# Attention units with key blocks turned by VectorE and DMA: another sharing-out of copies, exponentials and scores

## The chip, the cores and the metric

The kernel runs on one core of a Trainium2 chip. The core has a matrix engine (TensorE, "PE" in the profile, with "PEld" for its weight loads), VectorE ("DVE"), ScalarE ("ACT"), GpSimd ("POOL") and SyncE ("SP"), which here issues every DMA. Each engine works through its own instructions in program order; semaphores tie them together. TensorE writes to PSUM, eight banks of 512 float32 columns on 128 partitions; VectorE and ScalarE read it back.

The metric is the device time of one execution in microseconds (us). Before the change the median of three runs is 2802.39 us (2792.26 to 2804.34).

## What is computed

An encoder layer over a context of 77 tokens, then a decoder layer over x, which has 2 batches of 2048 tokens with 512 channels. The change concerns the decoder's causal self-attention with 16 heads of 32 channels:

```python
yn = _ln(y, dec_n1_s, dec_n1_b)
y = y + _mha(yn, yn, dec_sa_in_w, dec_sa_in_b, dec_sa_out_w, dec_sa_out_b, sb)
...
scores = jnp.einsum('bhqd,bhkd->bhqk', q, k) / jnp.sqrt(jnp.asarray(hd, xq.dtype))
scores = scores + bias[None]
attn = jax.nn.softmax(scores, axis=-1)
out = jnp.einsum('bhqk,bhkd->bhqd', attn, v)
```

`sb` is a relative-position bias plus a causal mask; keys after the query have no weight. Everything is float32.

## The kernel before

The self-attention is cut into 128 **units** (b, m, g, t): batch b (2), token block m of 512 (4), head group g of four heads (4), query tile t of 128 (4), in this order. A unit has n = 4m + t + 1 key blocks of 128. These are grouped into *pieces* of at most four blocks (`pieces`, L315). For each piece the following happens:

- **Scores** (`scores`, L391). Four matmuls, one per head, into four PSUM banks (L409). VectorE evicts each into the large buffer `pp` and takes a running maximum (L422; L429 for the two blocks near the diagonal, with the bias). After a unit's last piece one reduction (L439) gives the negative maxima `nm`, and four exponentials, one per head over the unit's whole width, are put on a list, `late_exps`. They are issued later by `exps(k)` (L364) on ScalarE (L444, in place, with a sum).
- **Turning** (`turn`, L450). The probabilities have queries on the partitions; for the product with the values the keys must be there. TensorE transposes each key block's four heads into one bank (L466), and VectorE (L474) or ScalarE (L476) copies the bank into one of the `pts` tiles.
- **Values** (`values`, L483). One matmul per key block and head (L503) adds up the unit's output in one bank, which is then copied (ScalarE, L517) or added (VectorE, L519) to `oT`.

Units for which `moved(n)` (L332) holds turn their first piece (the *far* one, four key blocks) in another way. These are all units of m = 3 and of block (1, 2), but for the last two of all. `move_out` (L378) transposes squares of 32 x 32 within `pp` on VectorE, with two instructions (L383) that cover the four heads, and writes the result to DRAM with two DMAs (L384, tensor `turn`). `move_in` (L386) reads it back with four DMAs (L389) into `landing`, the upper half of `pts_all`, in an order that completes the transposition. `move(n)` calls `move_out` and gives the space free for later scores. TensorE does not transpose these four blocks.

The order of work is written out by hand in the loop at the end of `tile_encoder_decoder`. It goes through the units and, within a unit, through its *visits* (`visits_of`, L336): one or two pieces of a unit that isn't moved; one piece of a moved one, with the far blocks' values in the last visit. So a moved unit of m = 3 has three visits and one of (1, 2) has two. In a visit the loop turns the piece, runs at the unit's end the next `slot` (projections, norms and output products of neighbouring blocks, weight loads, GpSimd work), moves the next unit's far piece out (`early`), issues exponentials, scores up to two pieces of units n + 1 and n + 2, and then the values; the landing DMAs come last. `stream` lists the pieces still to be scored, in order; `may_score` tells whether the next one's space in `pp` is free. Units of even and odd number use opposite ends of `pp`, so unit n + 2 writes where unit n was.

PSUM banks are handed out in a ring (`bank`, eight banks); `values` takes the oldest one for its sums and puts it back at the end. So a matmul may have to wait for the eviction of whatever used the bank eight calls earlier.

Which engine copies a turned bank is decided by `half` (L470 to L472): in a moved unit of m = 3 the fourth copy of a piece (o == 3) goes to VectorE; in one of (1, 2) the second half of each piece; all others to ScalarE. The exponentials of the next unit are issued for m = 3 as two in the first visit, two in the second and none in the third; for (1, 2) all four in the first visit.

After the attention, `ff_slot` and `cross` run the cross-attention and the feed-forward layers, whose matmuls (L1686, L1715 and others) fill the rest of the time.

Of the kernel before, what the change touches and what calls it, by code (L numbers as in the profile page):

```python
# [22 lines left out]
HC = P // HD  # L23
MB = 512
NMB = T // MB
# [29 lines left out]
def tile_encoder_decoder(ctx: ExitStack, tc: tile.TileContext, ins, out):  # L55
# [103 lines left out]
    with (  # L159
# [169 lines left out]
        units = [(b, m, g, t) for b in range(B) for m in range(NMB) for g in range(NC) for t in range(TB)]  # L329
        stream = [(n, k0, kn) for n, u in enumerate(units) for k0, kn in pieces(u[1] * TB + u[3])]  # L330

        def moved(n):  # L332

            return (units[n][1] == NMB - 1 or units[n][:2] == (1, 2)) and n < len(units) - 2

        def visits_of(n):  # L336

# [26 lines left out]
        def exps(k):  # L364

            for _ in range(min(k, len(late_exps))):
                late_exps.pop(0)[1]()
# [82 lines left out]
        def turn(pieces):  # L450

            first = units[pieces[0][0]][1] == 0
            loads = []
            for n, k0, kn in pieces:
                ks = range(k0, k0 + kn)
                if first:
                    heads = [(n, k, r) for r in range(HC) for k in ks]
                    loads += [heads[o : o + TB] for o in range(0, len(heads), TB)]
                else:
                    loads += [[(n, k, r) for r in range(HC)] for k in ks]  # L460
            for o, load in enumerate(loads):
                pt = bank()
                pts = in_turn("pts4", pts_all[:, :HC]) if moved(pieces[0][0]) else in_turn("pts", pts_all)
                pts = pts.rearrange("p (x q) -> p x q", q=P)
                for x, (n, k, r) in enumerate(load):
                    nc.tensor.transpose(pt[:, ts(x, P)], state[n]["p"][r][:, k], ident)  # L466
                    got[n, k, r] = pts[:, x, :]
                w = len(load) * P
                free = pieces[0][0] == len(units) - 2 and (pieces[0][1] or o >= 4)
                half = o >= (len(loads) + 1) // 2  # L470
                if moved(pieces[0][0]) and units[pieces[0][0]][1] == NMB - 1:
                    half = o == 3  # L472
                if free or (o % 2 if first else o in (4, 6) if len(loads) == 8 else half):
                    nc.vector.tensor_copy(pts[:, : len(load), :], pt[:, :w])  # L474
                else:
                    nc.scalar.copy(pts[:, : len(load), :], pt[:, :w])  # L476
                if not first and o == (7 if len(loads) == 8 else min(3, len(loads) - 1)):
                    exps(1)
            exps(HC if first else 0 if units[pieces[0][0]][1] == NMB - 1 else 1)

        sums_held = {}

        def values(n, turned, far, opens, ends):  # L483
            b, m, g, t = units[n]
            for k0, kn in far:
                parts = landing.rearrange("p a (r k x) -> p r k a x", r=HC, x=RB)
                for k in range(kn):
                    for r in range(HC):
                        got[n, k0 + k, r] = parts[:, r, k]
            ks = [k for k0, kn in turned + far for k in range(k0, k0 + kn)]  # L490
            whole = m == 0
            key = (b, m, g) if whole else n
            begun = key in sums_held
# [1436 lines left out]
        def score_next():  # L1930
            score_at()
            at[0] += 1
# [29 lines left out]
        for n, visit, turned, far in ((n, k, *w) for n in range(end) for k, w in enumerate(visits_of(n))):  # L1962
            pair = [(n, *p) for p in turned]
            while scored_to[n] != size[n]:
                score_next()
            while any(u == n for u, _ in late_exps):
                exps(1)
            ends = visit == len(visits_of(n)) - 1
            if moved(n) and n not in gone:
                move(n)  # L1970
                move_in(n)
            turn(pair)
            if n == end - 2:
                for _, k0, _ in pair:
                    feed(k0 + 4)
            leave(n, turned)
            turned_to[n] += sum(kn for _, kn in turned)
            third = units[n][1] == 2
            if third and ends:
                exps(2)  # L1980
            if ends and n + 1 < end:
                slot(n + 1)
            early = ends and n + 1 < end and moved(n + 1)
            early = early and scored_to[n + 1] == size[n + 1] and not any(u == n + 1 for u, _ in late_exps)
            if early:
                move(n + 1)
            if not third:
                exps((0, 2, 1, 1)[units[n][1]])
            if moved(n):
                for _ in range(2):  # L1990
                    if may_score() and stream[at[0]][0] <= n + 2:
                        score_next()
            elif may_score():
                if units[n][1] and (len(pair) > 1 or third):
                    score_two()
                else:
                    score_next()
            if third and not ends:
                exps(1)
            values(n, turned, far, visit == 0, ends)  # L2000
            if early:
                move_in(n + 1)
            while not moved(n) and may_score() and (len(pair) > 1 or units[n][1] == 0):
                score_next()
            if third and not ends:
                exps(1)
# [68 lines left out]
```

## Time and profile before

| | |
|---|---|
| median of three runs | 2802.39 us |
| the profiled execution: its time / its span | 2802.98 us / 2801.1 us |
| TensorE busy | 2725.2 us (97%) |
| VectorE busy | 1893.3 us (68%) |
| ScalarE busy | 1483.3 us (53%) |
| copies of turned banks on ScalarE (L476) / on VectorE (L474) | 614 / 290 |
| moving out: VectorE transposes (L383) / DMAs out / DMAs in | 92 / 92 / 184 |
| granted TensorE clock, mean | 0.989 |

A row of a group reads: line, engine, operation, output <- input, shape, count | busy us, mean ns of one | idle us of that engine just before these instructions, and what ended most of it. "DVE pp L422" as a releaser means VectorE's instruction of line 422 that writes `pp`. A matmul's busy time includes its place in the pipeline; a full PE row is therefore not yet a TensorE at its peak. In the view of stretches each row gives a window in us from the span's start, its length, then busy us (and instructions) of PE, PEld, DVE, ACT and POOL, the granted TensorE clock, the DMA engines' share and GB/s. In a timeline a row gives start us, length us, engine, line, operation and count, and in brackets the idle time before it with its releaser. In the view of waits it is who <- for whom: us in total, times, longest.

### The profile page before, as it was taken

How to read it: one execution, taken by the hardware profiler on the slowest of the kernel's cores; microseconds unless marked ns; L12 is line 12 of the kernel's file. 1: busy time of each engine (PE TensorE's matmuls, PEld its weight loads, DVE VectorE, ACT ScalarE, POOL GpSimd, SP SyncE). 2: the span in 40 equal slices, each digit the busy share in tenths (PEclk: the TensorE clock that was granted, in tenths of full speed). 3: DMA queues.
4: the chain of work that ended last, by engine and by line, in shares of the span. 5: the costliest groups of instructions: out<-in, count | busy, mean ns of one | idle time of the engine just before them, and what ended most of it. 6: DMA issues, size and time to landing. Idle time of an engine off the chain costs nothing. (4 is left out here: it accounts for less than half of the span.)

```text
span 2801.1 us, 67173 instructions
## 1 busy us (share of the span) xinstructions
PE 2725.2 (97%) x25870; PEld 2172.0 (78%) x25870; DVE 1893.3 (68%) x5481; ACT 1483.3 (53%) x2878; POOL 1000.8 (36%) x844
## 2 busy tenths in 40 slices
PE   9999999999999999988989999999999999999998
PEld 5678777766666677766666767898989898989898
DVE  4776688878885677778888785464655655564645
ACT  3545567756676556745556676435343444444431
POOL 3512145400301513313300011374647474747455
PEclk9999999999999999999999999999999999999999
DMA  8735355435555522368874565574758575757575
GB/s 236 209 90 148 110 176 162 134 105 161 173 163 157 146 70 75 109 197 243 248 192 143 149 192 181 167 245 142 241 145 243 165 235 159 225 161 222 147 226 184
DMA packets 347792, 481.50 MB, mean 172 GB/s; under 512 B 45600, under 2 KB 170064, under 8 KB 347346
## 3 DMA queue, kind: packets, MB, share of 16 engines
q1 hardware_dynamic: 347474, 477.22, 57.8%
q8 instruction: 205, 3.36, 0.5%
q14 instruction: 113, 0.93, 0.1%
HBM read 382.39 MB, written 94.71 MB: 170 GB/s over the span
## 5 line engine op out<-in xcount | busy, mean ns | idle before, releaser
L444 ACT ACTIVATE pp<-pp,nm 128x128 f32<-128x128 f32 (+15 forms) x512 | 611.7, 1200 | 53.6 <-DVE nm L439 50.6
L422 DVE TENSOR_SCALAR_CACHE_REDUCE pp<-psum 128x512 f32<-128x512 f32 (+3 forms) x1024 | 555.1, 590 | 58.4 <-DMA turn<-pp 30.3
L476 ACT COPY pts<-psum 128x512 f32<-128x512 f32 x614 | 328.6, 594 | 386.1 <-PE psum L466 353.7
L466 PE MATMUL psum<-ident,pp 128*128 128x128 f32 x3616 | 461.8, 280 | 8.3 <-ACT nT L310 4.0
L466 PEld LDWEIGHTS psum<-ident,pp 128*128 128x128 f32 x3616 | 398.7, 143 | 67.1 <-issue 36.0
L409 PE MATMUL psum<-kT,q 32*128 32x512 f32 (+3 forms) x2560 | 402.2, 566 | 10.2 <-DVE pp L422 3.9
L503 PEld LDWEIGHTS psum<-pts,vv 128*32 128x32 f32 x8704 | 229.1, 112 | 182.5 <-DVE pp L422 86.1
L503 PE MATMUL psum<-pts,vv 128*32 128x128 f32 x8704 | 298.6, 281 | 37.2 <-DVE pp L422 31.2
L1715 PE MATMUL psum<-pp 128*128 128x128 f32 x2560 | 304.5, 276 | 1.9 <-POOL pp L1010 1.6
L1715 PEld LDWEIGHTS psum<-pp 128*128 128x128 f32 x2560 | 296.3, 192 | 8.6 <-issue 3.0
L409 PEld LDWEIGHTS psum<-kT,q 32*128 32x128 f32 x2560 | 172.9, 184 | 148.8 <-issue 53.5
L1010 POOL TENSOR_TENSOR pp<-pp 128x512 f32<-128x512 f32 x159 | 212.6, 1353 | 112.0 <-ACT pp L862 45.5
L1686 PE MATMUL psum<-vv,pp 128*128 128x256 f32 x1024 | 236.2, 381 | 0.0
L474 DVE COPY pts<-psum 128x512 f32<-128x512 f32 x290 | 191.5, 685 | 61.1 <-PE psum L466 60.5
L1686 PEld LDWEIGHTS psum<-vv,pp 128*128 128x128 f32 x1024 | 190.3, 190 | 25.8 <-issue 0.5
L429 DVE CUSTOM_DVE_ANT_0 pp<-psum,bias 128x256 f32<-128x256 f32 (+1 forms) x512 | 195.6, 410 | 16.6 <-PE psum L409 16.6
L1699 DVE TENSOR_TENSOR kT<-kT,psum 128x512 f32<-128x512 f32 x96 | 65.8, 687 | 191.1 <-PE psum L1686 190.9
L1686 PE MATMUL psum<-nT,pp 128*128 128x256 f32 x768 | 174.1, 380 | 0.0
L1702 ACT ACTIVATE kT<-kT,vecs 128x256 f32<-128x256 f32 x192 | 87.0, 501 | 156.6 <-DVE kT L1699 155.9
L542 POOL TENSOR_TENSOR oT<-rirows,oT 128x512 f32<-128x512 f32 x30 | 38.4, 1280 | 361.1 <-DMA rirows<-rec 245.4
L1686 PEld LDWEIGHTS psum<-nT,pp 128*128 128x128 f32 x768 | 144.2, 190 | 20.3 <-issue 1.6
L1723 ACT COPY oT<-psum 128x128 f32<-128x128 f32 x56 | 15.0, 268 | 238.8 <-PE psum L1715 238.8
(273 smaller groups left out, 4229.3 us busy)
## 6 DMA issues: line engine op xcount, KB each, us to landing
pp<-w_d SPq DMA_DIRECT2D x520, 256.0 KB
turn<-pp SPq DMA_DIRECT2D x92, 512.0 KB
pts<-turn SPq DMA_DIRECT2D x184, 256.0 KB
pp<-in_dec_ff_wT_dram SPq DMA_DIRECT2D x112, 256.0 KB
bias<-tzg SPq DMA_DIRECT2D x128, 128.0 KB
pp<-wo_d SPq DMA_DIRECT2D x56, 256.0 KB
wqk<-in_dec_sa_in_wT_dram SPq DMA_DIRECT2D x52, 256.0 KB
wqk<-sa_q SPq DMA_DIRECT2D x84, 128.0 KB
```

What stands on the lines that cost most here:

```text
L409: nc.tensor.matmul(banks[r][:, : kn * P], q[rows4(r), ts(t, P)], kT[rows4(r), g, k0 * P : (k0 + kn) * P], start=True, stop=True,)
L422: nc.vector.tensor_scalar(to, got_s, 1.0, None, ALU.mult, ALU.max, accum_out=st["mx"][:, r, c : c + 1],)
L429: nc.vector.tensor_tensor_reduce(p[:, k0 + far : i + 1], s[:, far:kn], near[:, 2 - (kn - far) :], 1.0, LOWEST, ALU.add, ALU.max, accum_out ...
L444: nc.scalar.activation(p, p, AF.Exp, bias=nm, accum_out=to)
L466: nc.tensor.transpose(pt[:, ts(x, P)], state[n]["p"][r][:, k], ident)
L474: nc.vector.tensor_copy(pts[:, : len(load), :], pt[:, :w])
L476: nc.scalar.copy(pts[:, : len(load), :], pt[:, :w])
L503: nc.tensor.matmul(o if len(p.shape) == 2 else o.rearrange("p (a x) -> p a x", x=RB), vv[:, k, ts(g * HC + r, HD)], p, start=k == ks[0] an ...
L1010: engine.tensor_tensor(out, a, b, ALU.subtract)
L1686: nc.tensor.matmul(mm[:, ts(f, TOK)], a[:, c, ts(f, P)], b[:, c, :], start=fresh and f == 0 and c == 0, stop=c == 1, skip_group_check=True,)
L1702: nc.scalar.activation(dst[:, e, :], src[:, e, :], AF.Relu, bias=vec("dec_ff1_b", f + e))
L1715: nc.tensor.matmul(psum[:, bank_i, ts(col, P)], lhs[:, c, :], w[:, c, :], start=fresh and k in (0, 3) and c == 0, stop=c == 3, skip_group_ ...
```

## The change

Four units are no longer moved (`OPEN`: the first two of block (0, 3) and the first two of block (1, 2)). In moved units ScalarE copies every turned bank (`half = False`). A visit's values take the far blocks first. In a moved unit's visits the loop has a branch of its own: exponentials go one per visit from `turn`, with the rest (`exps(HC)`) at the unit's end, and in (1, 2) one more behind each visit's values; if the next piece to score is a unit's first, its second goes ahead of it where space allows; the next unit's far piece is moved out before these scores in (1, 2) and after them at m = 3. A unit that isn't moved but precedes a moved one (`then`) moves that one's far piece out just before its own values.

```diff
+        OPEN = ((0, NMB - 1, 0, 0), (1, 2, 0, 0))
+
         def moved(n):
 
-            return (units[n][1] == NMB - 1 or units[n][:2] == (1, 2)) and n < len(units) - 2
+            b, m, g, t = units[n]
+            return (m == NMB - 1 or (b, m) == (1, 2)) and n < len(units) - 2 and (b, m, g, t // 2) not in OPEN
...
-                if moved(pieces[0][0]) and units[pieces[0][0]][1] == NMB - 1:
-                    half = o == 3
+                if moved(pieces[0][0]):
+                    half = False
...
-            exps(HC if first else 0 if units[pieces[0][0]][1] == NMB - 1 else 1)
+            exps(HC if first else 0 if units[pieces[0][0]][1] == NMB - 1 or moved(pieces[0][0]) else 1)
...
-            ks = [k for k0, kn in turned + far for k in range(k0, k0 + kn)]
+            ks = [k for k0, kn in far + turned for k in range(k0, k0 + kn)]
...
+            if moved(n):
+                if ends:
+                    exps(HC)
+                    slot(n + 1)
+                early = ends and moved(n + 1)
+                if early:
+                    assert scored_to[n + 1] == size[n + 1] and not any(u == n + 1 for u, _ in late_exps)
+                if early and third:
+                    move(n + 1)
+                for _ in range(2):
+                    if at[0] == len(stream) or stream[at[0]][0] > n + 2:
+                        break
+                    if stream[at[0]][1] == 0 and may_score(1) and stream[at[0] + 1][0] == stream[at[0]][0]:
+                        stream[at[0] : at[0] + 2] = stream[at[0] + 1], stream[at[0]]
+                    if may_score():
+                        score_next()
+                if early and not third:
+                    move(n + 1)
+                values(n, turned, far, visit == 0, ends)
+                if early:
+                    move_in(n + 1)
+                if third:
+                    exps(1)
+                continue
...
-            if moved(n):
-                for _ in range(2):
-                    if may_score() and stream[at[0]][0] <= n + 2:
-                        score_next()
-            elif may_score():
+            if may_score():
...
+            then = ends and not early and n + 1 < end and moved(n + 1) and scored_to[n + 1] == size[n + 1]
+            if then and not any(u == n + 1 for u, _ in late_exps):
+                early = True
+                move(n + 1)
             values(n, turned, far, visit == 0, ends)
...
-            while not moved(n) and may_score() and (len(pair) > 1 or units[n][1] == 0):
+            while may_score() and (len(pair) > 1 or units[n][1] == 0):
                 score_next()
```

One unit of m = 3 (unit 53) as the loop writes it out before and after. T4 is the turning of key block 4, with A or D for the copying engine; E54 an exponential of unit 54; S55[4+4] the scores of unit 55's four blocks from the fourth on; V the values; OUT and IN the moving:

```
before: T4A T5A T6A T7D E54 E54 S55[0+4] S55[4+4] V | T8A T9A T10A T11D E54 E54 S55[8+4] V | T12A T13A slot OUT54 S55[12+4] V IN54
after:  T4A T5A T6A T7A E54 S55[4+4] S55[0+4] V | T8A T9A T10A T11A E54 S55[8+4] V | T12A T13A E54 E54 slot S55[12+4] OUT54 V IN54
```

And one of (1, 2) (unit 101):

```
before: T4A T5A T6D T7D E102 E102 S103[0+4] S103[4+4] E102 V E102 | T8A T9D slot OUT102 S103[8+4] V IN102
after:  T4A T5A T6A T7A E102 S103[4+4] S103[0+4] V E102 | T8A T9A E102 slot OUT102 S103[8+4] V IN102 E103
```

## The prediction

> **What bounds the kernel now.** First the page's head and its slices, to see where TensorE is not full:
>
> ```profile
> PE 2725.2 (97%) x25870; PEld 2172.0 (78%) x25870; DVE 1893.3 (68%) x5481; ACT 1483.3 (53%) x2878; POOL 1000.8 (36%) x844
> PE   9999999999999999988989999999999999999998
> DVE  4776688878885677778888785464655655564645
> ```
>
> TensorE dips below nine tenths in slices 18, 19 and 21 of 40 (1190 to 1470 us, a slice being 70 us), with VectorE at seven and eight tenths. From the 26th on (about 1750 us) it is full to the end: feed-forward matmuls, which can only start when the attention is over, so what the attention saves or loses moves the end one for one. The attention has 128 units (one L439 per unit); I cut the span at every fourth or sixteenth L439. The view of stretches gives, in order: block (0,2), whose units move nothing; the first four units of (0,3); its next eight; the first four of (1,2); its other twelve; block (1,3).
>
> ```profile
> core 0: us, PE busy (x) PEld busy (x) DVE busy (x) ACT busy (x) POOL busy (x), PEclk, DMA share, GB/s
> 362.30:578.20 215.90, 215.80 (x2600) 168.14 (x2598) 177.72 (x608) 157.21 (x274) 94.74 (x79) 1.00 0.51 149
> 578.20:658.00 79.80, 72.97 (x795) 52.44 (x794) 59.88 (x186) 47.98 (x71) 1.27 (x1) 0.96 0.42 121
> 658.00:801.20 143.20, 138.72 (x1622) 97.17 (x1621) 118.63 (x379) 101.60 (x157) 28.21 (x22) 1.00 0.60 172
> 1197.50:1262.00 64.50, 54.63 (x577) 39.61 (x577) 48.96 (x150) 33.25 (x55) 10.19 (x9) 0.92 0.65 198
> 1262.00:1445.30 183.30, 165.05 (x1786) 119.62 (x1785) 156.80 (x481) 98.88 (x168) 49.51 (x39) 0.94 0.81 235
> 1445.30:1658.90 213.60, 203.69 (x2373) 145.10 (x2372) 174.32 (x550) 140.77 (x208) 18.96 (x15) 0.98 0.58 164
> ```
>
> Blocks (0,2) and (1,2) have the same tokens, heads and keys, and (1,2) spares TensorE the turning of 4 key blocks in each unit. Yet it takes 64.5 + 183.3 = 247.8 us against 215.9. Where blocks are moved, VectorE is the fullest engine that does not pipeline: 156.80 of 183.3 (86%), 118.63 of 143.2 (83%). The groups of the same stretches (first the eight units of (0,3), then the twelve of (1,2)) say what fills it and what TensorE waits for:
>
> ```profile
> L422 DVE TENSOR_SCALAR_CACHE_REDUCE pp<-psum 128x512 f32<-128x512 f32 (+3 forms) x112 | 64.2, 628 | 5.8 <-DMA turn<-pp 4.6 <-PE psum L409 1.2
> L444 ACT ACTIVATE pp<-pp,nm 128x1664 f32<-128x1664 f32 (+3 forms) x32 | 58.9, 1849 | 3.6 <-DVE nm L439 3.6
> L476 ACT COPY pts<-psum 128x512 f32<-128x512 f32 x68 | 35.6, 597 | 33.1 <-PE psum L466 31.6 <-ACT pp L444 0.9 <-ACT oT L517 0.6
> L474 DVE COPY pts<-psum 128x512 f32<-128x512 f32 x16 | 11.0, 685 | 1.8 <-PE psum L466 1.8
> L383 DVE STREAM_TRANSPOSE pp<-pp 128x1024 f32<-128x1024 f32 x16 | 18.9, 1220 | 0.9 <-ACT pp L444 0.9
> L503 PEld LDWEIGHTS psum<-pts,vv 128*32 128x32 f32 x928 | 23.7, 109 | 19.2 <-DVE pp L422 10.2 <-issue 6.8 <-ACT pts L476 2.2
> ...
> L422 DVE TENSOR_SCALAR_CACHE_REDUCE pp<-psum 128x512 f32<-128x512 f32 (+3 forms) x124 | 68.8, 607 | 16.3 <-DMA turn<-pp 12.3 <-PE psum L409 2.4 <-PE psum L466 1.7
> L444 ACT ACTIVATE pp<-pp,nm 128x1152 f32<-128x1152 f32 (+3 forms) x48 | 67.6, 1410 | 10.0 <-DVE nm L439 8.5 <-DMA turn<-pp 1.5
> L476 ACT COPY pts<-psum 128x512 f32<-128x512 f32 x41 | 22.4, 584 | 57.8 <-PE psum L466 49.5 <-DVE pp L383 4.2 <-issue 4.0
> L474 DVE COPY pts<-psum 128x512 f32<-128x512 f32 x36 | 23.6, 684 | 2.8 <-PE psum L466 2.8
> L429 DVE CUSTOM_DVE_ANT_0 pp<-psum,bias 128x256 f32<-128x256 f32 x48 | 18.7, 417 | 0.0
> L383 DVE STREAM_TRANSPOSE pp<-pp 128x1024 f32<-128x1024 f32 x24 | 28.3, 1219 | 0.6 <-ACT pp L444 0.6
> ```
>
> The values (L503) wait for VectorE's evictions of scores (L422), and VectorE itself stands still until the DMA that carries moved blocks out has read the space it writes to (12.3 us of 183.3).
>
> **The change, part by part.** The sum is made against the profiled execution, 2802.98 us (span 2801.1; the median of three runs is 2802.39, lowest 2792.26).
>
> *(a) All copies of turned pieces to ScalarE.* Going through the loop visit by visit, L474 falls from 290 copies to 199 and L476 rises from 614 to 721; in the 42 units still moved VectorE loses 98. That is 8 per four units of blocks m = 3 (11.0 / 2 = 5.5 us of VectorE) and 12 per four of (1,2) (23.6 / 3 = 7.9 us). ScalarE gains 8 x 0.597 = 4.8 and 12 x 0.584 = 7.0 us.
> [...]
>
> *(b) Scores in another order.* When a unit's first piece is next, its second goes ahead, so the eviction into moved-out space comes one piece (four L422 of 607 ns, 2.4 us) later. The waits of the whole run, with count and longest:
>
> ```profile
> DVE pp L422 <- DMA turn<-pp: 30.3, 18, 3.8
> ```
>
> One lasts 30.3 / 18 = 1.7 us. I take the waits as gone: 4.6 / 2 = 2.3 us per four units at m = 3, 12.3 / 3 = 4.1 in (1,2). Between nothing and all, all is nearest, as a piece's delay is as long as most waits.
>
> *(c) m = 3: what VectorE's 5.5 + 2.3 = 7.8 us are worth.* There are 28 moved units in (0,3) and (1,3), seven groups of four at 71.6 us (143.2 / 2). If all is passed on, 7 x 7.8 = 55 us; if none, 0. ScalarE, the receiver, had 101.60 of 143.2 and gets 16 x 0.597 = 9.6: 111.2, or 13.9 us per unit where a unit takes 17.9; VectorE falls to 118.63 - 11.0 = 107.6, 13.5 per unit. Both have room, but with more waits between them. I take 60%: -33 us. (The L503 row's waits on VectorE and ScalarE, 12.4 us in eight units, show that not all of 15.6 lay on TensorE's path.)
> Exponentials come one, one and two per visit, behind the copies, and the moving-out (two L383, 2.4 us) stands behind the last of them, so VectorE will wait there more than the 0.9 us of now. In exchange it comes after the score evictions: the values no longer wait for it. I set these two against each other at nothing; if the cover fails, the second rival gives the price. The DMAs go with it: each unit's two writes wait for L383 in SP's queue, and behind them stand the four landings and the next slot's loads.
>
> ```profile
> SPq L384 <- DVE pp L383: 215.2, 60, 12.6
> SPq L389 <- DMA turn<-pp: 107.3, 82, 4.9
> ```
>
> SP waits there already (3.6 us each time), and weights are asked for three jobs, over a unit, ahead; one piece's evictions later costs nothing as long as that lead holds, and up to the 2.5 us of a piece per unit without it (28 x 2.5 = 70, part of the second rival's direction). Moved values ahead of the turned ones in the last visit add no instruction; their data landed a visit ago, and the last copy gets time to finish: within the 60%.
>
> *(d) (1,2): a ring through ScalarE.* Here the end of each visit issues one exponential. The one at the unit's end needs the maxima (L439) of scores that VectorE evicts behind the moving-out, which waits for the previous exponential; behind it in ScalarE's queue stand the next unit's copies, behind these its values. Such a passage today:
>
> ```profile
> 1396.04 2.36 DVE L383 STREAM_TRANSPOSE pp<-pp 128x1024 f32<-128x1024 f32 x2
> ...
> 1399.79 0.17 DVE L439 TENSOR_REDUCE nm<-mx 128x4 f32<-128x12 f32 x1
> ...
> 1399.99 1.36 ACT L444 ACTIVATE pp<-pp,nm 128x1280 f32<-128x1280 f32 x1 [0.46 <-DVE nm L439]
> ```
>
> The ring for one unit: four exponentials 67.6 / 12 = 5.6; 6.5 copies of 22.4 / 41 = 0.55, 3.6; an output copy, 0.25; two L383, 2.36; the unit's last pieces (15 of 42 key blocks in four units; evictions (68.8 + 18.7) / 3 = 29.2 per four, so 10.4 / 4 = 2.6); L439 0.17 and two hand-overs, about 0.3. Sum 14.9, or 59.5 per four, against 61.1 now (183.3 / 3). Low end, if the ring isn't felt: VectorE's 7.9 + 4.1 = 12.0 less per four, 3.5 groups, -42. High end: VectorE's other work of the slot (156.80 - 68.8 - 18.7 - 23.6 - 28.3 = 17.4, or 5.8 per four) falls into the ring: 65.3, +4.2 each, +15. A ring without any further wait is too good; I take 62, +3 us in all.
>
> *(e) The openings.* Units 48, 49, 96 and 97 are no longer moved. Now the first unit of (1,2) moves out at its own visit and the weights for the next projection come behind that in SP's queue:
>
> ```profile
> 590.00:620.00 30.00, 23.20 (x199) 15.73 (x201) 16.01 (x42) 11.64 (x17) 0.00 (x0) 0.89 0.46 137
> 1210.00:1240.00 30.00, 20.16 (x192) 13.19 (x184) 17.70 (x53) 10.37 (x17) 0.00 (x0) 0.83 0.74 222
> 1220.00:1230.00 10.00, 5.00 (x16) 3.31 (x20) 1.21 (x3) 0.00 (x0) 0.00 (x0) 0.50 0.65 222
> ...
> 1215.82 1.67 PE L1182 MATMUL psum<-wqk,xr 128*128 128x256 f32 x7
> 1225.00 3.75 PE L1182 MATMUL psum<-wqk,nT 128*128 128x256 f32 x8 [7.51 <-DMA wqk<-in_dec_sa_in_wT_dram]
> L466 PE MATMUL psum<-ident,pp 128*128 128x128 f32 x3616 | 461.8, 280 | 8.3 <-ACT nT L310 4.0 <-DVE pp L422 3.2 <-DVE wbig L1198 0.2
> ```
>
> TensorE idles 30 - 20.16 = 9.8 us at the one and 6.8 at the other. Against it stand 64 more transposes of 461.8 / 3616 = 0.128, 8.2 us (VectorE saves eight L383, 9.8; six DMAs per unit fall away). 16.6 - 8.2 = 8.4, and eight matmuls at half clock took 3.75 instead of 1.9, with the like at 600: some 3.5 more. -12; from -4 (the stall moves to units 50 and 98) to -20.
> [...]
>
> Sum: -33 + 3 - 12 = -42: 2803 - 42 = **2761 us**.
>
> **The rivals.** *First, full passage* (chance 0.16): VectorE alone sets the pace and the ring isn't felt: -55 - 42 - 12 = -109, **2694**, and up to 2735 where it holds for (1,2) or for m = 3 alone. For it: 86% VectorE, and (0,2) at 215.9. Against: 13.9 us of ScalarE per unit.
> *Second, slower* (0.13): the ring through ScalarE closes at m = 3 too: ScalarE's 13.9, then the moving-out 2.36 and one piece's evictions 2.6 before it can go on, 18.9 against 17.9: 28 x 1.0 = +28; (1,2) +15; openings -12: +31, **2834**. It decides from where VectorE waits before each pair of L383 for over 1 us more than the copies free (5.5 / 4 = 1.4), so over 2.4 us a unit, and ScalarE waits before its copies for VectorE and no longer for TensorE. For it: all four exponentials now stand behind copies. Against: at m = 3 the next unit's first copies and exponential depend on neither.
> *Third, no gain beyond the openings* (0.13): freed VectorE time is waited away, at m = 3 and in (1,2) at once: -12 + 3 = -9, 2794. For it: VectorE already idles 24.6 of 143.2 us. That the reordering seldom acts is out: 35 units get their second piece ahead that did not before.
>
> **How the numbers follow.** Forecast 0.58 with its own range 2735 to 2785. About 0.5% (14 us) is what a measurement of this kernel tells from no change. Faster by more: 0.58 + 0.16 = 0.74; within: 0.13; slower: 0.13. The range leaves out the slower case (0.13) and the deeper end of the first rival (0.07): 2712 to 2802.
>
> **What would show it.** L474 at 199 and L476 at 721; L383 at 84; "DVE pp L422 <- DMA turn<-pp" near nothing; four units of (0,3) at 67 us instead of 71.6, of (1,2) near 62; no TensorE gap over 3 us near 595 or 1217. I am wrong if ScalarE's waits for L439 swell to several us per unit outside (1,2), or if m = 3 stays at 71.6.

## The result, and the profile after

The changed kernel takes **2836.42 us** (median of four runs, 2834.10 to 2838.66) against 2803.36 us for the kernel before (2792.26 to 2805.57): a ratio of 1.0126, 95% interval 1.0097 to 1.0155. It is slower; the forecast was 2761 us, with a range up to 2802. The profiled execution took 2834.1 us with a span of 2832.3. The kernel before was run again beside each group of experiments below, with medians of 2803.67, 2801.89 and 2803.15 us.

The page of the changed kernel, first its head, then the groups that answer to the ones of before:

```profile
PE 2751.9 (97%) x25934; PEld 2188.2 (77%) x25934; DVE 1835.2 (65%) x5380; ACT 1538.2 (54%) x2985; POOL 1001.0 (35%) x844
...
L447 ACT ACTIVATE pp<-pp,nm 128x128 f32<-128x128 f32 (+15 forms) x512 | 614.5, 1206 | 106.1 <-DVE nm L442 89.7
L425 DVE TENSOR_SCALAR_CACHE_REDUCE pp<-psum 128x512 f32<-128x512 f32 (+3 forms) x1024 | 558.7, 590 | 106.6 <-PE psum L412 76.6
L479 ACT COPY pts<-psum 128x512 f32<-128x512 f32 x721 | 382.9, 594 | 264.4 <-PE psum L469 232.9
L469 PE MATMUL psum<-ident,pp 128*128 128x128 f32 x3680 | 480.4, 284 | 23.4 <-ACT pp L447 10.4
...
L412 PE MATMUL psum<-kT,q 32*128 32x512 f32 (+3 forms) x2560 | 406.2, 574 | 25.5 <-DVE oT L522 11.9
...
L477 DVE COPY pts<-psum 128x512 f32<-128x512 f32 x199 | 129.9, 685 | 43.3 <-PE psum L469 42.7
```

Lines of the changed kernel stand three higher than before: L447 is the exponential that was L444, L469 the transposes, L412 and L425 the scores and their eviction. The copies moved as counted: 199 on VectorE, 721 on ScalarE, and VectorE's busy time fell by 58 us. What is new is in the last column. ScalarE's exponentials waited 89.7 us for the maxima (L442), and TensorE now waits for exponentials (10.4 us) and for the output's addition on VectorE (L522, 11.9 us).

Stretches cut at the same units as in the prediction: the first four units of (0,3), its next eight, all its rest up to the last unit, the first four and the other twelve of (1,2), and (1,3) up to the last but one.

```profile
core 0: us, PE busy (x) PEld busy (x) DVE busy (x) ACT busy (x) POOL busy (x), PEclk, DMA share, GB/s
573.40:647.70 74.30, 69.65 (x811) 53.11 (x810) 55.58 (x183) 47.84 (x71) 1.28 (x1) 0.93 0.23 65
647.70:800.80 153.10, 142.56 (x1620) 98.79 (x1619) 110.58 (x362) 111.03 (x175) 28.25 (x22) 0.94 0.55 160
647.70:850.10 202.40, 189.09 (x2195) 129.12 (x2194) 148.66 (x491) 149.20 (x233) 29.53 (x23) 0.96 0.56 163
1202.20:1261.80 59.60, 55.69 (x601) 41.33 (x601) 44.80 (x146) 35.55 (x59) 10.54 (x9) 0.97 0.46 144
1261.80:1465.10 203.30, 185.31 (x1786) 131.88 (x1783) 136.69 (x445) 116.39 (x205) 49.45 (x39) 0.89 0.72 212
1465.10:1735.90 270.80, 252.53 (x2936) 173.82 (x2933) 197.85 (x655) 192.60 (x289) 19.03 (x15) 0.96 0.53 150
```

The two longer stretches of before, for the same cuts:

```profile
658.00:850.80 192.80, 185.59 (x2197) 128.01 (x2194) 160.33 (x515) 137.06 (x210) 29.49 (x23) 1.00 0.60 174
1445.30:1706.10 260.80, 247.71 (x2944) 175.06 (x2943) 214.39 (x685) 175.99 (x261) 18.96 (x15) 0.98 0.56 156
```

| us | before | after | difference |
|---|---|---|---|
| (0,3), first four units | 79.8 | 74.3 | -5.5 |
| (0,3), the rest | 192.8 | 202.4 | +9.6 |
| (1,2), first four units | 64.5 | 59.6 | -4.9 |
| (1,2), the other twelve | 183.3 | 203.3 | +20.0 |
| (1,3) | 260.8 | 270.8 | +10.0 |
| sum | 781.2 | 810.4 | +29.2 |

That is 29.2 of the 31.2 us by which the span grew. So the openings gained (10.4 us), both kinds of moved unit lost, and the stretch with the largest loss is the one the prediction had put at +3. In it TensorE's idle time did not grow (18.3 us before, 18.0 after); its busy time did, by 20.3 us for the same 1786 matmuls, and the granted clock fell from 0.94 to 0.89.

**What waits in (1,2).** The groups of the twelve units, 1261.8 to 1465.1 us:

```profile
L425 DVE TENSOR_SCALAR_CACHE_REDUCE pp<-psum 128x512 f32<-128x512 f32 (+3 forms) x124 | 69.7, 607 | 23.3 <-PE psum L412 13.3 <-DMA turn<-pp 9.7 <-issue 0.2
L447 ACT ACTIVATE pp<-pp,nm 128x1152 f32<-128x1152 f32 (+3 forms) x48 | 68.6, 1429 | 62.9 <-DVE nm L442 62.8
...
L386 DVE STREAM_TRANSPOSE pp<-pp 128x1024 f32<-128x1024 f32 x24 | 28.4, 1219 | 3.5 <-ACT pp L447 3.5
L412 PEld LDWEIGHTS psum<-kT,q 32*128 32x128 f32 x292 | 28.0, 187 | 28.3 <-ACT pts L479 14.5 <-issue 4.6 <-DVE mx L432 3.2
```

The last of these rows in the kernel before, for its twelve units:

```profile
L409 PEld LDWEIGHTS psum<-kT,q 32*128 32x128 f32 x294 | 23.6, 184 | 21.2 <-DVE pp L422 4.6 <-issue 4.0 <-DVE mx L429 3.8
```

ScalarE stands 62.8 us, 5.2 per unit, in front of an exponential whose maxima are not there; before it was 8.5. Copies are queued behind that exponential, and the score matmuls wait for a bank that one of these copies must empty (14.5 us, a releaser that their row of before does not name among its three). The timeline of one such passage (start, length, engine, line, operation, count, idle time before):

```profile
1395.53 3.53 PE L412 MATMUL psum<-kT,q 32*128 32x512 f32 x8 [0.53 <-ACT pts L479]
...
1404.62 1.27 ACT L447 ACTIVATE pp<-pp,nm 128x1152 f32<-128x1152 f32 x1
...
1407.58 0.76 DVE L1201 TENSOR_TENSOR kT<-psum,kT 128x256 f32<-128x256 f32 x2 [7.24 <-PE psum L1185]
...
1408.25 2.36 DVE L386 STREAM_TRANSPOSE pp<-pp 128x1024 f32<-128x1024 f32 x2
...
1411.38 1.76 PE L412 MATMUL psum<-kT,q 32*128 32x512 f32 x8
...
1412.00 0.17 DVE L442 TENSOR_REDUCE nm<-mx 128x4 f32<-128x12 f32 x1
...
1412.20 1.36 ACT L447 ACTIVATE pp<-pp,nm 128x1280 f32<-128x1280 f32 x1 [5.50 <-DVE nm L442]
1413.56 1.54 ACT L479 COPY pts<-psum 128x512 f32<-128x512 f32 x3
...
1414.18 1.40 PE L506 MATMUL psum<-pts,vv 128*32 128x128 f32 x24 [1.03 <-ACT pts L479]
```

The last exponential of a unit ends at 1405.9. VectorE could move the unit out then, but a projection's addition of the slot (L1201) stands ahead in its queue and waits for TensorE; so the moving-out begins 2.4 us later, the next maxima come at 1412.2, the exponential after 5.5 us of waiting, and only behind it the copies for which the values (L506) wait.

**What waits at m = 3.** The eight units of (0,3), 647.7 to 800.8 us:

```profile
L425 DVE TENSOR_SCALAR_CACHE_REDUCE pp<-psum 128x512 f32<-128x512 f32 (+3 forms) x112 | 65.0, 630 | 19.6 <-PE psum L412 12.4 <-DMA turn<-pp 4.7 <-PE psum L469 2.3
L447 ACT ACTIVATE pp<-pp,nm 128x2048 f32<-128x2048 f32 (+3 forms) x33 | 61.4, 1869 | 0.1
L469 PE MATMUL psum<-ident,pp 128*128 128x128 f32 x336 | 46.1, 290 | 4.6 <-DVE pp L425 2.4 <-ACT pp L447 1.4 <-ACT nT L310 0.6
...
L386 DVE STREAM_TRANSPOSE pp<-pp 128x1024 f32<-128x1024 f32 x16 | 18.9, 1219 | 0.7 <-ACT pp L447 0.7
L412 PEld LDWEIGHTS psum<-kT,q 32*128 32x128 f32 x256 | 17.4, 187 | 22.3 <-issue 8.1 <-DVE oT L522 7.2 <-ACT nT L310 3.0
```

The transposes and the weight loads of the scores in the same units before:

```profile
L466 PE MATMUL psum<-ident,pp 128*128 128x128 f32 x336 | 42.8, 278 | 0.1
L409 PEld LDWEIGHTS psum<-kT,q 32*128 32x128 f32 x257 | 20.6, 183 | 17.9 <-issue 6.3 <-DVE pp L422 5.4 <-DVE mx L429 2.3
```

ScalarE's exponentials wait here for nothing (0.1 us), and VectorE hardly before its moving-out (0.7). VectorE has 8.1 us less to do than before and spends it waiting for scores: its evictions waited 1.2 us for L409, now 12.4 for L412. TensorE in turn waits for L522, which stands behind the moving-out in VectorE's queue and empties the bank of the values, and for exponentials. Over the whole run, in the view of waits (who <- for whom: us, times, longest):

```profile
PEld psum L412 <- DVE oT L522: 26.5, 22, 2.4
...
PEld psum L469 <- ACT pp L447: 14.2, 16, 1.8
...
DVE pp L425 <- DMA turn<-pp: 23.3, 23, 4.3
```

The waits for the DMA out, which the new order of scores was to remove, fell from 30.3 us in 18 times only to 23.3 in 23.

### The profile page after: what moved, and what is told of

Its sections match the earlier page's. It is cut to its first block, busy times and chain, and to the rows that moved or that the text cites. A ratio compares the mean times of both kernels' runs of the same rounds, so it can differ in the third digit from the quotient of the medians.

```text
span 2832.3 us, 67301 instructions
## 1 busy us (share of the span) xinstructions
PE 2751.9 (97%) x25934; PEld 2188.2 (77%) x25934; DVE 1835.2 (65%) x5380; ACT 1538.2 (54%) x2985; POOL 1001.0 (35%) x844
## 5 line engine op out<-in xcount | busy, mean ns | idle before, releaser
L447 ACT ACTIVATE pp<-pp,nm 128x128 f32<-128x128 f32 (+15 forms) x512 | 614.5, 1206 | 106.1 <-DVE nm L442 89.7
L425 DVE TENSOR_SCALAR_CACHE_REDUCE pp<-psum 128x512 f32<-128x512 f32 (+3 forms) x1024 | 558.7, 590 | 106.6 <-PE psum L412 76.6
L479 ACT COPY pts<-psum 128x512 f32<-128x512 f32 x721 | 382.9, 594 | 264.4 <-PE psum L469 232.9
L469 PE MATMUL psum<-ident,pp 128*128 128x128 f32 x3680 | 480.4, 284 | 23.4 <-ACT pp L447 10.4
L469 PEld LDWEIGHTS psum<-ident,pp 128*128 128x128 f32 x3680 | 414.3, 145 | 86.3 <-issue 33.5
L412 PE MATMUL psum<-kT,q 32*128 32x512 f32 (+3 forms) x2560 | 406.2, 574 | 25.5 <-DVE oT L522 11.9
L506 PEld LDWEIGHTS psum<-pts,vv 128*32 128x32 f32 x8704 | 235.5, 114 | 168.5 <-DVE pp L425 66.4
L506 PE MATMUL psum<-pts,vv 128*32 128x128 f32 x8704 | 307.0, 287 | 18.4 <-DVE pp L425 8.3
L412 PEld LDWEIGHTS psum<-kT,q 32*128 32x128 f32 x2560 | 166.9, 185 | 168.2 <-issue 56.7
L477 DVE COPY pts<-psum 128x512 f32<-128x512 f32 x199 | 129.9, 685 | 43.3 <-PE psum L469 42.7
```

Source lines behind the costliest of these rows:

```text
L412: nc.tensor.matmul(banks[r][:, : kn * P], q[rows4(r), ts(t, P)], kT[rows4(r), g, k0 * P : (k0 + kn) * P], start=True, stop=True,)
L425: nc.vector.tensor_scalar(to, got_s, 1.0, None, ALU.mult, ALU.max, accum_out=st["mx"][:, r, c : c + 1],)
L447: nc.scalar.activation(p, p, AF.Exp, bias=nm, accum_out=to)
L506: nc.tensor.matmul(o if len(p.shape) == 2 else o.rearrange("p (a x) -> p a x", x=RB), vv[:, k, ts(g * HC + r, HD)], p, start=k == ks[0] an ...
```

## The experiments

Three theories. *Late exponentials:* one exponential per visit, put behind the copies, is what costs: at the end of (1,2)'s units it closes the ring, at m = 3 it makes the next unit's transposes late. *Copies:* ScalarE has no room for all of them. *Place of the moving-out:* behind the scores it holds up VectorE's queue. Each experiment changes only an order, the engine of some copies, or which units are moved. Medians stand with the ratio to the kernel before and its interval.

**1. No exponential behind the last values in (1,2)** (changed kernel)

```diff
-                if third:
+                if third and not ends:
                     exps(1)
```

> The changed kernel, but in block (1,2) no exponential is issued behind the values of a unit's last visit; it goes into the next visit instead. Ring theory (ScalarE holds the next unit's copies behind an exponential that waits for maxima): ScalarE's waits for the reduction L442 inside (1,2), 62.8 us in twelve units, fall below 15; those twelve units go from 203.3 us back to some 183 to 187; the whole from 2836 to about 2818. Copy theory (the loss comes from ScalarE alone copying all turned banks): the twelve units stay over 198 and the whole within 8 us of 2836.

2805.63 us (1.0012, 1.0000 to 1.0024): 31 us less than the changed kernel, more than expected. Its exponentials on the page, and the stretch of (1,2)'s twelve units:

```profile
L447 ACT ACTIVATE pp<-pp,nm 128x128 f32<-128x128 f32 (+15 forms) x512 | 614.0, 1205 | 30.1 <-DVE nm L442 29.2
```

```profile
1259.20:1436.80 177.60, 159.35 (x1776) 117.89 (x1772) 136.09 (x445) 115.91 (x202) 49.57 (x39) 0.94 0.83 243
```

The wait for the maxima falls from 89.7 to 29.2 us (in the twelve units from 62.8 to 2.6) and the stretch from 203.3 to 177.6; the score matmuls' wait for a copy is no longer among the first three of their row there. The instructions are the same; one instruction's place makes 25.7 us. The ring is shown.

This run also tells how far two profiled executions of the same order differ. Up to (1,2) its instructions stand as in the changed kernel, and yet the rest of (0,3) takes 198.0 us here and 202.4 there.

**2. All exponentials where they were before** (changed kernel; m = 3 two, two and none, (1,2) all four in the first visit)

```diff
-            exps(HC if first else 0 if units[pieces[0][0]][1] == NMB - 1 or moved(pieces[0][0]) else 1)
+            exps(HC if first else 0 if units[pieces[0][0]][1] == NMB - 1 else 1)
...
+                if not third:
+                    exps(1)
                 early = ends and moved(n + 1)
...
+                if third and not ends:
+                    exps(1)
                 values(n, turned, far, visit == 0, ends)
...
-                if third:
+                if third and not ends:
                     exps(1)
```

> The changed kernel with its exponentials where they stood before: m = 3 two, two and none per visit, (1,2) all four in the first visit. If late exponentials are the cause in both places: the ring's 20 us and the 24 us by which the moved units of m = 3 grew both go, 2836 to about 2793. Copy theory: (1,2) may gain, m = 3 keeps at least 15 of its 24 us, the whole over 2812.

2785.94 us (0.9934, 0.9913 to 0.9955): 50 us less than the changed kernel and 18 less than before. By stretch against the changed kernel: (1,2)'s twelve units 173.0 (-30.3), the rest of (0,3) 198.1 (-4.3), (1,3) 261.2 (-9.6). The first run, which still has the late exponentials in these two blocks, took 198.0 and 271.3 us there: so the 4.3 us in (0,3) are not shown to come from the exponentials, the 10 us in (1,3) are. On the page the transposes no longer wait for exponentials first:

```profile
L469 PE MATMUL psum<-ident,pp 128*128 128x128 f32 x3680 | 467.8, 280 | 11.8 <-DVE pp L425 6.1
...
L412 PE MATMUL psum<-kT,q 32*128 32x512 f32 (+3 forms) x2560 | 393.8, 568 | 22.2 <-DVE oT L522 11.8
```

The second row still has its wait for L522; that belongs to the third theory.

**3. Copies shared as before** (changed kernel)

```diff
-                if moved(pieces[0][0]):
-                    half = False
+                if moved(pieces[0][0]) and units[pieces[0][0]][1] == NMB - 1:
+                    half = o == 3
```

> The changed kernel with the copies shared out as before (VectorE takes the fourth copy of a piece at m = 3 and the second half of each piece in (1,2)). Copy theory: m = 3 goes back to about 71.6 us per four units from 75 to 77, the whole to about 2805 to 2812. Exponential theory: ScalarE's ring in (1,2) loses 3 copies of 0.55 us per unit, at most 20 us; m = 3 stays over 74; the whole 2816 to 2836.

2812.94 us (1.0038, 1.0024 to 1.0052): 23 us less than the changed kernel, of which 14.7 in (1,2)'s twelve units (188.6). The eight units of (0,3) stay at 149.1 / 2 = 74.6 us per four, as the theory of the late exponentials had it, while the time lies between the two forecasts. With fewer copies behind the late exponential its lateness costs less, as far as (1,2) tells. Copies on ScalarE cost something here, but whether by themselves this run can't say.

**4. The openings alone** (kernel before, with `OPEN` and `then`)

```diff
-            return (units[n][1] == NMB - 1 or units[n][:2] == (1, 2)) and n < len(units) - 2
+            b, m, g, t = units[n]
+            return (m == NMB - 1 or (b, m) == (1, 2)) and n < len(units) - 2 and (b, m, g, t // 2) not in ((0, NMB - 1, 0, 0), (1, 2, 0, 0))
...
+            then = ends and not early and n + 1 < end and moved(n + 1) and scored_to[n + 1] == size[n + 1]
+            if then and not any(u == n + 1 for u, _ in late_exps):
+                early = True
+                move(n + 1)
```

> The kernel before with the four opening units no longer moved, and the rule that lets an unmoved unit move its successor out; nothing else. Both theories: the two openings give the 10.6 us that the changed kernel's first groups show (79.9 to 74.3, 64.6 to 59.6), and nothing is lost elsewhere: about 2792. If the stall only moves to units 50 and 98: 2800 or more.

2801.39 us (0.9987, 0.9972 to 1.0002): about 2 us, not distinguishable from none. The first four units of the blocks take 78.0 and 56.4 us (-1.8 and -8.1), but the units behind them 196.4 and 185.8 (+3.6 and +2.5): more than half of the gain is given back at once.

**5. The second run with the scores in the order of before**

```diff
-                    if stream[at[0]][1] == 0 and may_score(1) and stream[at[0] + 1][0] == stream[at[0]][0]:
-                        stream[at[0] : at[0] + 2] = stream[at[0] + 1], stream[at[0]]
```

> The kernel of the second run (exponentials as before) and the scores in their old order too. Against 2786. If the new order does what the prediction's term (b) says: VectorE's waits for the moved blocks' DMA (DMA turn) come back, some 10 to 20 us longer, near 2800. If the order is what keeps m = 3 some 5 us over the kernel before: 2780 or less, and the rest of (0,3) (units 52 to 63) falls from 198 to near 193 us.

2862.32 us (1.0219, 1.0202 to 1.0236): 76 us more than the second run, and far more than either theory had.

```profile
L425 DVE TENSOR_SCALAR_CACHE_REDUCE pp<-psum 128x512 f32<-128x512 f32 (+3 forms) x1024 | 555.8, 590 | 178.1 <-DMA turn<-pp 114.4
```

The waits for the DMA out are 114.4 us instead of 28.6 in the second run: with the moving-out behind the scores the DMA comes later, and the first piece of the next scores would run into it. So the new order is needed, but at m = 3 mostly to undo what the later moving-out does: the seventh run, with the old order and the moving-out ahead of the scores, waits 52.4 us. In (1,2) the moving-out keeps its place, and there the new order is worth 11.4 us by itself (173.0 us for the twelve units in the second run, 184.4 here; VectorE's waits for the DMA out in them 13.9 and 30.5 us).

**6. The second run with the moving-out ahead of the scores at m = 3 too**

```diff
-                if early and third:
+                if early:
                     move(n + 1)
...
-                if early and not third:
-                    move(n + 1)
```

> The kernel of the second run, and at m = 3 the moving-out stands before the scores again, as in the kernel before and in (1,2). Bank theory (a score matmul waits for the bank whose sum VectorE adds, L522, and that add now stands behind the moving-out): PEld's waits L412 <- L522 at m = 3, 8.4 us in units 52 to 59, vanish, and the rest of (0,3) goes from 198 to near 193, (1,3) down by about as much: 2776 to 2780. If the move's place is neutral or good, as the prediction has it: 2786 or more.

2774.98 us (0.9903, 0.9888 to 0.9918), 11 us less than the second run, with (0,3)'s rest at 190.4 us and (1,3) at 254.2. The score row on its page:

```profile
L412 PE MATMUL psum<-kT,q 32*128 32x512 f32 (+3 forms) x2560 | 386.3, 566 | 12.7 <-DVE pp L425 6.8
```

The wait for L522 is no longer its first releaser, and the row's idle time falls from 22.2 to 12.7 us. VectorE's waits for the DMA out fall as well, from 28.6 to 16.4 us, so the run does not tell what each of the two is worth.

**7. The copies alone** (kernel before)

```diff
-                if moved(pieces[0][0]) and units[pieces[0][0]][1] == NMB - 1:
-                    half = o == 3
+                if moved(pieces[0][0]):
+                    half = False
```

> The kernel before with ScalarE copying every turned bank of moved units, and nothing else. The prediction's term (a) by itself: VectorE loses 98 copies, 5.5 us per four units at m = 3 and 7.9 in (1,2); by 60% of it some 2803 - 35 = 2768. Copy theory after the third run (which gained 23.5 us by going back): VectorE's time is not what TensorE waits for, ScalarE's is: 2800 to 2815.

2807.32 us (1.0024, 1.0012 to 1.0036): 3 to 10 us *more* than before. All 46 units are still moved here, so it is 107 copies that change their engine (721 on ScalarE instead of 614), not 98. VectorE's work falls from 1893.3 to 1831.4 us on the page, and the view of its waits says where most of the 62 us went:

```profile
DVE pp L422 <- DMA turn<-pp: 52.4, 23, 5.0
DVE pp L422 <- PE psum L409: 48.5, 52, 3.3
```

Before these were 30.3 and 25.1 us, together 45 less. A VectorE with less to do comes to the moved-out space earlier and waits longer for the DMA, and for scores. The sixth run, 32 us faster, has the same copies and the same places of the exponentials and of the moving-out; it differs by the openings, by the values' order and by the new order of scores, and its waits for the DMA out are 16.4 us instead of 52.4.

**8. The second run with (1,2) not moved**

```diff
-            return (m == NMB - 1 or (b, m) == (1, 2)) and n < len(units) - 2 and (b, m, g, t // 2) not in OPEN
+            return m == NMB - 1 and n < len(units) - 2 and (b, m, g, t // 2) not in OPEN
```

> The kernel of the second run with block (1,2) not moved at all, so that TensorE turns 14 x 16 more squares of 0.128 us, 29 us of its time, and the DMAs of 14 units fall away. If a moved unit of (1,2) still pays more in waits than it saves: (1,2) goes from 57.9 + 173.0 = 230.9 us to the 216 of the unmoved (0,2), the whole to about 2771. If moving pays once the exponentials are early: 2795 or more.

2775.63 us (0.9901, 0.9887 to 0.9916), 10 less than the second run. Block (1,2) takes 52.1 + 164.0 = 216.1 us, the time of (0,2), where moved with early exponentials it took 57.9 + 173.0 = 230.9.

**9. The changed kernel with the moving-out ahead of the scores at m = 3** (the edit of the sixth run, exponentials left late)

> The changed kernel (late exponentials) with the moving-out before the scores at m = 3. Bank theory: what the order cost at early exponentials, 11 us, is won here too, 2836 to about 2825. Rival: with the last exponentials issued at the unit's end, the moving-out now holds VectorE, and the scores behind it, until ScalarE is done; that is why it was put behind them: 2836 or more, with VectorE's waits L386 <- ACT L447 several times the 2 to 5 us of the changed kernel at m = 3.

2874.07 us (1.0248, 1.0230 to 1.0265): 38 us more than the changed kernel, where the same edit had gained 11 with early exponentials. In the view of waits VectorE now stands in front of the moving-out, for 61.8 us instead of 12.5:

```profile
DVE pp L386 <- ACT pp L447: 61.8, 22, 5.4
```

So the later moving-out was the right place for late exponentials. The two had to be moved together, and early is better for both.

**10. The sixth run with the copies shared as before** (the edit of the third run)

> The kernel of the sixth run (2775: exponentials as before, moving-out first, new score order, openings) with the copies shared out as before. Copy theory: TensorE waits for copies, so the sharing gains as in the third run: about 2755 to 2765. If copies only hurt because they stood before late exponentials: within 5 us of 2775, or worse by VectorE's 5.5 to 7.9 us per four units, up to 2800.

2768.31 us (0.9873, 0.9859 to 0.9888). That is 7 us less than the sixth run by the medians; the intervals of the two only just touch, and the two profiled spans differ by 1.2 us, so a small gain at most.

**11. The sixth run with (1,2) not moved** (the edit of the eighth run)

> The kernel of the sixth run with block (1,2) not moved. (1,2) from 226.9 to 216 us, as the eighth run showed: 2764 to 2767. If the two gains overlap: 2772 or more.

2764.96 us (0.9860, 0.9846 to 0.9875): (1,2) takes 216.1 us against 226.9, but (1,3) 261.0 against 254.2.

**12. Nothing moved** (kernel before)

```diff
-            return (units[n][1] == NMB - 1 or units[n][:2] == (1, 2)) and n < len(units) - 2
+            return False
```

> The kernel before with no unit moved at all. TensorE turns 46 x 16 more squares (94 us of its time), VectorE is rid of 92 transposes (112 us) and of the DMAs. If moving only makes waits: (1,2) as (0,2), 216 us, and the blocks of m = 3 about 255 to 260 each, the whole 2745 to 2765. If it pays at m = 3: over 2790.

**2730.32 us** (0.9736, 0.9721 to 0.9750), 73 us less than before and 106 less than the changed kernel: the best of all that ran, and better than expected. Its page, with the chain that ended last as second row:

```profile
PE 2709.4 (99%) x26606; PEld 2217.3 (81%) x26606; DVE 1840.3 (67%) x5445; ACT 1537.3 (56%) x2978; POOL 1001.1 (37%) x844
...
PE 93%; DMA 2%; ACT 1%; DVE 1%; POOL 1%; issue 1%; SPq 1%; DVEq 0%; POOLq 0%; ACTq 0%
...
L466 PE MATMUL psum<-ident,pp 128*128 128x128 f32 x4352 | 529.6, 277 | 4.7 <-ACT nT L310 4.0
```

Its stretches: (0,3)'s first four units, its rest, all of (1,2), and (1,3):

```profile
579.30:645.90 66.60, 66.56 (x832) 52.73 (x831) 55.99 (x186) 48.09 (x72) 1.28 (x1) 1.00 0.16 44
645.90:830.50 184.60, 184.18 (x2389) 143.98 (x2386) 151.24 (x508) 148.78 (x231) 29.47 (x23) 1.00 0.17 53
1177.60:1393.70 216.10, 216.00 (x2600) 168.26 (x2599) 177.64 (x607) 157.15 (x274) 60.45 (x48) 1.00 0.35 109
1393.70:1636.00 242.30, 242.16 (x3188) 192.34 (x3186) 203.22 (x679) 190.41 (x285) 19.00 (x15) 1.00 0.14 43
```

TensorE makes 736 transposes more (4352 against 3616), 67.8 us by their rows, and yet is busy 15.8 us less than before, with 0.7 us idle in these 709.6 and the full clock. Each of the three blocks is faster than in any moved form that ran.

## Why the prediction was wrong, point by point

**One error runs through the terms:** work that leaves a busy engine was priced as time, while the order in which the engines' queues hand over to each other was priced at nothing or nearly so.

- **(a) and the 60% of (c): refuted.** The prediction passed 60% of VectorE's freed time to the end, -33 us. The copies alone (seventh run) are worth between +3 and +10 us. "VectorE is the fullest engine" was read right (86% in (1,2)), but a full engine bounds only if its freed time reaches TensorE; here it turned into waits for the DMA and for scores (45 us more of them in the seventh run). Nor does it show a gain beside the new order of scores: the tenth run, which gives VectorE its copies back, is if anything faster than the sixth.
- **(b): right by itself, undone by the other parts.** The waits for the DMA out were taken as gone; 23.3 of 30.3 us remain. The new order of scores delays the eviction as foreseen: in (1,2), where the moving-out keeps its place, it is worth 11.4 us (fifth run) against the 12.3 of the prediction. But the moving-out behind the scores at m = 3 delays the DMA too, and (a) lets VectorE arrive earlier. The prediction named the moved DMAs and put their lateness at nothing as long as the weights' lead holds; in the fifth run it is the space in `pp` that pays (114.4 us).
- **(c) "I set these two against each other at nothing": this step failed.** The blocks of m = 3 were to gain 33 us and lost 19.6 (9.6 + 10.0), the largest miss of all; some 4 us of that lie within what two profiled executions differ by (first run). Late exponentials cost 10 us there, all of it in (1,3) (second run against the first), and the moving-out behind the scores another 11 (sixth run; 17.7 by the spans). The direction the prediction named, that the values no longer wait for the moving-out, was outweighed by what it did not name: the output's addition L522, now behind the moving-out, holds a bank that the next scores need. That m = 3 is slowed by both is shown by the runs; that it goes by L522 and by late transposes is read from the rows of waits, which come and go with the edits, and the later DMA out may have its part in it.
- **(d): the ring was right and mis-sized.** Forecast +3 with a bound of +15, both for 14 units; measured +20.0 in twelve. The sum of 14.9 us per unit was to be 15.5; it is 203.3 / 12 = 16.9. The high bound's reason, other work of the slot falling into the ring, is what the timeline shows (L1201 ahead of L386, 2.4 us); its 65.3 / 4 = 16.3 would have been the better choice. Taking the late exponential out of this place gives 25.7 us back.
- **(e): right by the stretch, wrong by the kernel.** -10.4 us in the eight opening units against the forecast -12; but alone the openings are worth 2 us (fourth run). The stall moves to the following units, the low end that the prediction had named as -4.

**The rivals.** The second rival's time, 2834 us, was met, but not its split or its mechanism. It asked for +28 at m = 3, by VectorE waiting over 2.4 us per unit ahead of the moving-out; that wait was 0.7 us in eight units, and m = 3 lost 19.6. It asked for +15 in (1,2) and got +20.0. The wait that it names, VectorE's in front of the moving-out, does appear in the ninth run, where the moving-out stands ahead of the scores at m = 3. The marker of the prediction's last paragraph, waits for the maxima "outside (1,2)", did not show either; "m = 3 stays at 71.6" was passed on the wrong side, at 153.1 / 2 = 76.6 us per four units. Of the third rival the mechanism holds for the copies, freed VectorE time that is waited away (seventh run), but not its price for the rest.

**The view that should have decided** was the prediction's own: (1,2) moved took 247.8 us, and (0,2), the same work not moved, 215.9. It served there only as a reason for the first rival. Read as what it is, it prices the moving, with the order of visits that goes with it, at 32 us in this block, before any reordering; the twelfth run finds 31.7 there (64.5 + 183.3 = 247.8 against 216.1) and 73 us in all.

**What stays open:** why late exponentials cost (1,3) 10 us and (0,3) nothing that shows; how the gain of the sixth run divides between L522 and the DMA out; and whether sharing the copies helps once the exponentials are early (tenth run). That (1,3) gets 6.8 us slower when (1,2) is not moved (eleventh run) can be narrowed down: 4.8 us of it lie in its first two units (44.8 us against 40.0 in the sixth run), where VectorE waits 3.7 us for the DMA out; the eighth run against the second shows the same (42.9 against 38.3).

## What to carry to other kernels

Time taken off a busy engine counts only where the wait behind it ends on the bound engine: of the 62 us taken off VectorE in the seventh run 45 came back as its waits, and the kernel was no faster. Before pricing it, ask what that engine will then wait for, and try that edit alone. An instruction that is moved to a place where its input is not ready holds up what stands behind it on its engine (ScalarE stood 62.8 us in front of such exponentials in twelve units, with copies behind them), so write the queue of each engine out and look for a ring through two of them; one place decided 26 us here. And where the profile holds the same work done in two ways, compare these two stretches before reordering either.

## What the runs showed of the hardware

**Stalls and a halved clock go together.** In the timeline above the eight score matmuls at 1395.53 take 3.53 us and the eight at 1411.38 take 1.76. A stretch that begins within the first:

```profile
1396.80:1401.80 5.00, 5.00 (x42) 3.01 (x41) 3.11 (x12) 2.19 (x5) 0.00 (x0) 0.50 1.04 240
```

The granted clock (third number from the end) is 0.50 there, with TensorE shown busy throughout. In windows of 0.25 us the twelve units after the change show a clock of 1.00 in 628 of 814 windows, of 0.50 in 169, and a mean between the two in 17; before it is 649, 75 and 10 of 734. Taking the clock as one of these two values at any time, an estimate from the means is that 2 x 0.11 of 203.3 us ran at half in (1,2) after the change and 2 x 0.06 of 183.3 before: 22.4 against 11.0 us lost, so up to some 11 of the 20.0 us are the clock's. With nothing moved the mean is 1.00 in all four stretches (twelfth run). In between, the mean in the twelve units is 0.91 at 188.6 us (third run), 0.94 at 177.6 (first) and 0.96 at 173.0 (second). That the stalls lower the clock, and not only go with it, is the author's reading of these rows; no run shows it by itself.

The stall ahead of that passage is short. The half clock begins at 1396.5 and lasts to 1403.3 us (0.50 in this window). In the 5 us ahead of it (clock 1.00) TensorE is shown busy for 4.47 us and the weight loads for 2.99; the idle time just before 1395.53 is 0.53 us for TensorE and 1.36 for the weight loads. The prediction counted the clock only as a gain, some 3.5 us at the openings.

**TensorE's idle time did not show these stalls.** (1,2) became 20.0 us longer with 18.0 us idle instead of 18.3; it is the busy time that grew. What showed the stalls was the idle time of the weight loads (PEld), 28.3 us instead of 21.2 for those of the scores, and the releasers there.

**ScalarE and VectorE kept the order of their queues in that passage.** The three banks that ScalarE copies at 1413.56 were filled by twelve transposes from 1409.93 on:

```profile
1409.93 1.53 PE L469 MATMUL psum<-ident,pp 128*128 128x128 f32 x12
```

These end at 1411.5, while ScalarE stands idle for 5.50 us in front of the exponential of 1412.20; the copies come 2.1 us later, behind it. So it is with VectorE's moving-out, whose input is there at 1405.9 and which begins at 1408.25, behind the addition (L1201) for which VectorE waited 7.24 us.
